# Moving the scale-and-round pass and the cap of a fake quantisation from VectorE to GpSimd in a chain of convolution layers

## The chip, the cores and the metric

The kernel runs on one core of a Trainium2 chip. The metric is the device time of one execution, in microseconds (us). The core has five engines that run side by side: TensorE (PE, with its weight loads shown as PEld), VectorE (DVE), ScalarE (ACT), GpSimd (POOL) and SyncE (SP), which here issues the DMAs. Each works through its own queue in order, and they wait for each other on semaphores.

## The reference, cut to what matters

The input is `x` of shape (4, 16, 512, 512). Four layers follow each other. Layer 0 is a windowed attention block. Layer 1 is what the change touches: its input is quantised with one step for the whole tensor, convolved, normalised with the mean and variance of the whole result, and clipped to 0..6.

```python
# layer 1
qp = 127.0
step = max(abs(x)) / qp
xq = clip(round(x / step), -qp, qp) * step
y = conv3x3(xq, wq)                       # wq is quantised in the same way
inv = gamma * rsqrt(var(y) + 1e-5)        # mean, var over batch, height, width
y = y * inv + (beta - mean(y) * inv)
y = clip(y, 0.0, 6.0)
# layer 2
out = conv3x3(relu(conv3x3(y, w1) + b1), w2) + b2 + y
# layer 3
out = out + w2 @ relu(w1 @ conv3x3(out) + b1) + b2
```

## The kernel before, in words

The image is cut into M = 64 pairs of rows per strip. A tile of the chain holds 128 partitions (4 strips or batches, 2 rows, 16 channels) by S = 4 by W = 512 fp32 elements, which is 2048 elements in each partition and 1 MiB in all.

The work has three stages. First, `window_attention` computes layer 0 and writes it to the DRAM tensor `x1`, in 64 steps. It also collects the largest absolute value in `peak`. Second comes the statistics pass at the head of `conv_layers` (L992 to L1014). Since layer 1 normalises with statistics of the whole convolution, its convolution is first computed for every tile only to collect them. Third comes the tail (the loop over `t` at the end of `conv_layers`), in which layers 1, 2 and 3 run as one pipeline, tile by tile, with the layer-1 convolution computed again.

In the statistics pass each of the 65 tiles (0 to 64) takes this path:

- `load` (L978; the DMAs at L891 to L895, issued by SP) brings the tile from `x1`. There are four buffers: two with the tag `x`, two with the tag `o`. A new load waits until the rounding has finished with the buffer.
- `scaled` (L984) multiplies the tile in place by the inverse step `ix` and adds `ROUND` = 12582912, which rounds to an integer in fp32.
- `rounded` (L987) subtracts `ROUND` on ACT and writes bf16 into one of three `qs` buffers.
- 24 turns of four matmuls (`_conv_turn`, L908) convolve tiles mm and mm+1 into four PSUM banks; two sets of banks alternate.
- `bn_stats` on DVE (L1009) reads the four banks.

Behind the last tile come the tiles -2 and -1 of the tail, whose first or last part lies outside the image and is set to zero by a memset (L888). Then `bn_aggr` (L1031) combines the statistics on DVE, and some ten tiny steps make `scale` and `shift` of it. Nothing of the tail's layer 1 can leave PSUM before.

In the tail one step `t` has four groups, each of them one convolution of 24 turns with the hidden layer of layer 3 (L1117, evacuated at L1123 on ACT and L1125 on DVE) laid between its turns, and the output product of layer 3 (L1131, L1137) at its end:

- group 1 is the convolution of layer 3, and between its turns the caps `clipped(t-1)` (L1060, one call per bank, with a memset at L1062 for tiles at the image's edge);
- group 2 is the second convolution of layer 2, and between its turns `scaled(t+2)` in four pieces of 512 elements, then `rounded(t+2)` in four;
- group 3 is the first convolution of layer 2, which reads the capped `z` of tiles t-2 and t-1;
- group 4 is the convolution of layer 1, after which `done0(t)` (L1054, ACT) writes `z` of tile t with scale, shift and ReLU. `done2` (L1084, DVE) later adds that `z` to the result of layer 2.

The order on PE, DVE, ACT and SP is the order in which the program text issues the instructions (a manual schedule, L961). POOL is not in that list: the framework's scheduler orders it. Before the change POOL holds a few memsets and three kinds of partition reduction, and nothing in the tail.

Of the kernel before, what the change touches and what calls it, by code (L numbers as in the profile page):

```python
# [14 lines left out]
ALU = mybir.AluOpType  # L15
# [20 lines left out]
ROUND = 12582912.0  # L36
BN_EPS = 1e-5
ACT_MAX = 6.0
# [813 lines left out]
def quant_step(nc, pool, out, columns, name):  # L852

    most = pool.tile([P, 1], F32, name=f"most_{name}")
    nc.vector.tensor_reduce(most, columns, AX.X, ALU.max, apply_absolute_value=True)
    every = pool.tile([P, 1], F32, name=f"every_{name}")
    nc.gpsimd.partition_all_reduce(every, most, P, bass_isa.ReduceOp.max)
    step = out.tile([P, 1], F32, name=f"step_{name}")
    nc.vector.tensor_scalar(step, every, 1.0 / QP, None, ALU.mult)
    inv = out.tile([P, 1], F32, name=f"inv_{name}")  # L860
    nc.vector.reciprocal(inv, step)
    return step, inv
# [17 lines left out]
def _quad(i):  # L880
    return slice(32 * i, 32 * i + 32)
# [34 lines left out]
def conv_layers(ctx: ExitStack, tc, x1, out, cw, cq, sw, m, v, peak):  # L916
# [18 lines left out]
    nc = tc.nc  # L935
# [33 lines left out]
    def inner(t):  # L969
        return t[:, :, 1 : W + 1]  # L970

    def outside(mm):

        return 0 if mm < 0 else S - 1 if mm >= M else None
# [6 lines left out]

    def scaled(mm, at=slice(0, S)):
        t = loaded[mm][:, at]
        nc.vector.tensor_scalar(t, t, ix, ROUND, ALU.mult, ALU.add)  # L984

    def rounded(mm, at=slice(0, S)):
        nc.scalar.activation(  # L987
# [7 lines left out]
    sx, ix = quant_step(nc, act, act, peak, "x")  # L995
    for mm in range(2):
        scaled(mm)
        rounded(mm)
    for mm in range(M):
        if mm + 4 <= M:  # L1000
            load(mm + 4, tags[mm % 2])
        if mm + 2 <= M:
            scaled(mm + 2)
            rounded(mm + 2)
        p = banks[4 * (mm % 2) : 4 * (mm % 2) + 4]
        for turn in _turns():
            _conv_turn(nc, p, cq, (qs(mm), qs(mm + 1)), *turn)
        for b in range(B):
            nc.vector.bn_stats(stats[:, mm * B + b, :], p[b])  # L1009
    for mm in (-2, -1):  # L1010
        load(mm)
        scaled(mm)
        rounded(mm)
# [43 lines left out]

    def clipped(mm, b):
        z = inner(zs(mm))
        nc.vector.tensor_scalar(z[:, b], z[:, b], ACT_MAX, None, ALU.min)  # L1060
        if outside(mm) is not None:
            nc.vector.memset(z[_quad(outside(mm)), b], 0.0)  # L1062

    def done1(mm):
        h = inner(hs(mm))
# [103 lines left out]
    for t in range(-2, M + 7):  # L1169
        if t + 3 <= M + 2:  # L1170
            load(t + 3)
        new = [lambda s=s: scaled(t + 2, slice(s, s + 1)) for s in range(S)]
        new += [lambda s=s: rounded(t + 2, slice(s, s + 1)) for s in range(S)]
        clip = [lambda b=b: clipped(t - 1, b) for b in range(B)]
        mm = t - 4
        group(
            conv(2, xs, mm - 1, done3, mm) if 0 <= mm <= M else None,
            (t - 6, 3) if 0 <= t - 6 < M else None,
            clip if -2 <= t - 1 <= M + 1 else [],
        )  # L1180
        mm = t - 3
        group(
            conv(1, hs, mm, done2, mm) if -1 <= mm <= M else None,
            (t - 5, 0) if 0 <= t - 5 < M else None,
            new if t + 2 <= M + 2 else [],
        )
        if -1 <= mm <= M:
            turned(mm)
        mm = t - 1
        group(  # L1190
            conv(0, zs, mm - 1, done1, mm) if -1 <= mm <= M + 1 else None,
            (t - 5, 1) if 0 <= t - 5 < M else None, [],
        )
        mm = t
        group(
            conv(None, qs, mm, done0, mm) if -2 <= mm <= M + 1 else None,
            (t - 5, 2) if 0 <= t - 5 < M else None, [],
        )
# [133 lines left out]
```

## Time and profile before

| what | value |
|---|---|
| median of three runs | 6609.31 us (6609.27 to 6616.03) |
| the profiled execution's own time | 6619.37 us |
| its span | 6617.5 us, mean granted clock 0.98 |
| PE busy | 6388.5 us, 97% of the span |
| ACT busy | 4209.4 us, 64% |
| DVE busy | 3192.7 us, 48% |
| POOL busy | 5.9 us |
| statistics pass | about 3560 to 3804 us in the span |
| tail | from there to the end |

The page of the profile cuts the span into 40 slices and shows for each the busy share of every engine in tenths. Rows of groups give the line of the kernel, the engine, the operation, the tiles (output <- input), their shapes, the number of instructions, busy time and mean duration of one in nanoseconds, and then the idle time of the engine before them with what ended it. Rows in order of time give the start and the duration. A row of busy time by stretch gives the stretch, its length, and each engine's busy time in it.

### The profile page before, as it was taken

How to read it: one execution, taken by the hardware profiler on the slowest of the kernel's cores; microseconds unless marked ns; L12 is line 12 of the kernel's file. 1: busy time of each engine (PE TensorE's matmuls, PEld its weight loads, DVE VectorE, ACT ScalarE, POOL GpSimd, SP SyncE). 2: the span in 40 equal slices, each digit the busy share in tenths (PEclk: the TensorE clock that was granted, in tenths of full speed). 3: DMA queues.
4: the chain of work that ended last, by engine and by line, in shares of the span. 5: the costliest groups of instructions: out<-in, count | busy, mean ns of one | idle time of the engine just before them, and what ended most of it. 6: DMA issues, size and time to landing. Idle time of an engine off the chain costs nothing. (4 is left out here: it accounts for less than half of the span.)

```text
span 6617.5 us, 317160 instructions
## 1 busy us (share of the span) xinstructions
PE 6388.5 (97%) x146976; PEld 3295.4 (50%) x146976; DVE 3192.7 (48%) x4640; ACT 4209.4 (64%) x5738; POOL 5.9 (0%) x25
## 2 busy tenths in 40 slices
PE   8999999999999999999996689999999999999998
PEld 5555555555555555555553344444444444444443
DVE  3444444444444444444445944444444444444444
ACT  5777777777777777777774545554555555555553
POOL 0000000000000000000000000000000000000000
PEclk9999999999999999999997789999999999999999
DMA  3333232333333333333324722222222222222221
GB/s 81 65 67 76 57 75 59 73 60 72 60 72 60 72 61 70 62 70 62 70 44 165 275 85 79 79 79 76 76 78 78 78 78 75 75 79 79 79 63 47
DMA packets 544391, 515.30 MB, mean 78 GB/s; under 512 B 349008, under 2 KB 480208, under 8 KB 514384
## 3 DMA queue, kind: packets, MB, share of 16 engines
q1 hardware_dynamic: 542768, 494.52, 28.6%
q8 instruction: 1154, 18.91, 1.2%
q14 instruction: 181, 1.48, 0.1%
q10 hardware_dynamic: 288, 0.39, 0.0%
HBM read 225.87 MB, written 134.48 MB: 54 GB/s over the span
## 5 line engine op out<-in xcount | busy, mean ns | idle before, releaser
L1117 PE MATMUL tb<-y,mat 32*32 32x512 f32 x16384 | 1684.6, 597 | 14.0 <-ACT hid L1123 7.5
L1123 ACT ACTIVATE hid<-tb,vec 128x512 f32<-128x512 f32 x1280 | 877.0, 687 | 1231.0 <-PE tb L1117 1205.6
L1125 DVE TENSOR_SCALAR hid<-tb,vec 128x512 f32<-128x512 f32 x768 | 576.8, 751 | 1173.9 <-PE tb L1117 860.5
L367 ACT ACTIVATE e<-pair 128x1024 f32<-128x1024 f32 x1024 | 992.4, 1021 | 225.7 <-PE pair L359 225.0
L295 PE MATMUL pair<-x,taps 32*32 32x512 f32 x18432 | 968.1, 606 | 1.9 <-ACT y L306 1.3
L416 PE MATMUL bank<-y,fc_e 32*32 32x512 f32 x8192 | 878.4, 607 | 3.7 <-ACT hid L421 3.1
L421 ACT ACTIVATE hid<-bank,f1b 128x512 f32<-128x512 f32 x1024 | 679.3, 686 | 298.3 <-PE bank L416 284.6
L351 DVE COPY yt<-bank 128x512 f32<-128x512 f32 x512 | 353.7, 691 | 905.8 <-PE bank L346 905.5
L1117 PEld LDWEIGHTS tb<-y,mat 32*32 32x32 f32 x16384 | 500.3, 103 | 406.0 <-issue 242.8
L359 PE MATMUL pair<-g,y 32*128 32x128 f32 x16384 | 652.2, 285 | 39.7 <-ACT e L367 38.7
L908 PE MATMUL tb<-z,cw 32*32 32x512 f32 x12864 | 643.8, 603 | 4.0 <-ACT z L1054 3.4
L359 PEld LDWEIGHTS pair<-g,y 32*128 32x128 f32 x16384 | 541.4, 186 | 185.9 <-ACT e L367 108.8
L908 PE MATMUL tb<-x,cw 32*32 32x512 f32 x12480 | 632.0, 597 | 1.5 <-ACT z L1054 1.5
L908 PE MATMUL tb<-h,cw 32*32 32x512 f32 x12672 | 628.6, 601 | 1.8 <-ACT z L1054 1.5
L295 PEld LDWEIGHTS pair<-x,taps 32*32 32x32 f32 x18432 | 459.0, 103 | 288.8 <-issue 183.7
L908 PE MATMUL tb<-q,cq 32*32 32x512 bf16 x12672 | 446.5, 436 | 122.1 <-ACT q L987 97.9
L378 PE MATMUL bank<-e,yt 128*32 128x128 f32 x16384 | 555.3, 276 | 0.9 <-ACT r L393 0.9
L383 PE MATMUL bank<-e,hot 128*32 128x512 f32 x4096 | 534.4, 592 | 0.0
L1131 PE MATMUL tb<-hid,mat 128*32 128x512 f32 x4096 | 498.5, 605 | 0.9 <-DVE o L1137 0.9
L378 PEld LDWEIGHTS bank<-e,yt 128*32 128x32 f32 x16384 | 417.7, 109 | 108.1 <-DVE yt L351 52.8
L429 DVE TENSOR_TENSOR xo<-bank,y 128x512 f32<-128x512 f32 x256 | 177.1, 692 | 546.2 <-PE bank L427 544.4
L346 PEld LDWEIGHTS bank<-mat,y 128*128 128x128 f32 x2048 | 215.2, 141 | 430.2 <-issue 376.5
(150 smaller groups left out, 6608.8 us busy)
## 6 DMA issues: line engine op xcount, KB each, us to landing
tx<-x SPq DMA_DIRECT2D x128, 1024.0 KB, 5.2
x<-in_xw_dram SPq DMA_DIRECT2D x32, 2600.0 KB, 9.9
y<-y SPq DMA_DIRECT2D x2048, 32.0 KB, 2.2
xi<-x SPq DMA_DIRECT2D x1024, 64.0 KB, 2.8
out_dram<-o SPq DMA_DIRECT2D x64, 1024.0 KB, 4.1
x<-xo SPq DMA_DIRECT2D x2000, 32.0 KB, 1.7
tx<-x SPq DMA_DIRECT2D x4, 768.0 KB, 4.2
x<-xo SPq DMA_DIRECT2D x48, 24.0 KB, 1.6
```

The costliest lines, as they stand in the source:

```text
L295: nc.tensor.matmul(bank(u)[quad(vv)], taps[quad(u), tap, :], xts[n // 2][quad(u), vv, dy : dy + WS, at : at + BW], start=tap == 0, stop=ta ...
L359: nc.tensor.matmul(bank(u)[:, P * jj : P * jj + P], y2[quad(u), vv, jl + jj].rearrange("p w t -> p (w t)"), g[quad(u), vv, jl + jj].rearra ...
L367: nc.scalar.activation(e[:, 2 * i : 2 * i + 2].rearrange("p u j t -> p u (j t)"), pairs[i], AF.Exp,)
L378: nc.tensor.matmul(b[quad(u), P * jj : P * jj + P], yt[:, jj, quad(u)], e[:, u, jj, :], start=True, stop=True,)
L383: nc.tensor.matmul(d[quad(u)], own, e[:, u].rearrange("p j t -> p (j t)"), start=True, stop=True,)
L416: nc.tensor.matmul(b[quad(k)], fc1[quad(vv), quad(k)], y[quad(vv), u, :], start=True, stop=True,)
L421: nc.scalar.activation(hd, b, AF.Gelu, bias=f1b)
L908: nc.tensor.matmul(p[i][_quad(j)], weights[_quad(i), side, dx, :], src[side][_quad(i), j, dx : dx + W], start=side == 0 and dx == 0, stop= ...
L1117: nc.tensor.matmul(p[_quad(c)], w1[_quad(b), 1 - par, 32 * c : 32 * c + 32], inner(ys(mm + par))[_quad(b), s, :], start=True, stop=True,)
L1123: nc.scalar.activation(hd, p, AF.Relu, bias=v("l3_b1"))
L1125: nc.vector.tensor_scalar(hd, p, v("l3_b1"), 0.0, ALU.add, ALU.max)
L1131: nc.tensor.matmul(out_bank[_quad(b), :], w2[:, par], hd, start=par == 0, stop=par == 1)
```

## The change

The scale-and-round pass of `scaled`, the cap of `clipped` and the memset behind the cap are issued on GpSimd. `scaled` serves both the statistics pass, with 2048 elements at a time, and the tail, with 512. Operands, types and the places in the program text stay as they were.

```diff
     def scaled(mm, at=slice(0, S)):
         t = loaded[mm][:, at]
-        nc.vector.tensor_scalar(t, t, ix, ROUND, ALU.mult, ALU.add)
+        nc.gpsimd.tensor_scalar(t, t, ix, ROUND, ALU.mult, ALU.add)
...
     def clipped(mm, b):
         z = inner(zs(mm))
-        nc.vector.tensor_scalar(z[:, b], z[:, b], ACT_MAX, None, ALU.min)
+        nc.gpsimd.tensor_scalar(z[:, b], z[:, b], ACT_MAX, None, ALU.min)
         if outside(mm) is not None:
-            nc.vector.memset(z[_quad(outside(mm)), b], 0.0)
+            nc.gpsimd.memset(z[_quad(outside(mm)), b], 0.0)
```

## The prediction

> **What bounds the kernel now.** I read the page's forty slices first, to see which stages there are, then busy time by stretch, then the groups and the order of time inside the stage that the change touches.
>
> ```profile
> PE   8999999999999999999996689999999999999998
> DVE  3444444444444444444445944444444444444444
> POOL 0000000000000000000000000000000000000000
> DMA  3333232333333333333324722222222222222221
> ```
>
> PE fills every slice but three, and only in those does VectorE (DVE) reach 9. They are the statistics pass. Busy time by stretch (engines in the order PE, PE weight load, DVE, ACT, POOL, then granted clock, DMA share, GB/s) puts figures on it:
>
> ```profile
> 3564.00:3576.00 12.00, 6.39 (x238) 3.86 (x238) 7.73 (x9) 6.09 (x4) 0.00 (x0) 0.57 1.01 422
> 3590.00:3790.00 200.00, 128.97 (x5308) 76.00 (x5284) 198.44 (x276) 110.27 (x55) 0.00 (x0) 0.77 0.82 292
> 3960.00:6500.00 2540.00, 2535.49 (x60055) 1113.48 (x60043) 1222.29 (x1939) 1282.62 (x1935) 0.00 (x0) 1.00 0.24 76
> ```
>
> In the pass (second row) DVE works 198.4 of 200 us and PE 129: DVE sets the pace. In the tail (third row) PE works 2535.5 of 2540 us and DVE under half: there a lighter DVE can give back at most the 4.5 us in which PE idles. The first row is the start of the pass, when four loads are waiting: DMA is full and moves 422 GB/s. The groups of the pass's steady part and two of its rounds in order of time:
>
> ```profile
> L1009 DVE BATCH_NORM_STATS2 stats<-tb 128x6 f32<-128x512 f32 x220 | 136.8, 684 | 1.6 <-PE tb L908 0.3
> L987 ACT ACTIVATE q<-tx,unround 128x2048 bf16<-128x2048 f32 x55 | 110.3, 2005 | 89.9 <-DVE tx L984 53.4 <-PE tb L908 36.5
> L984 DVE TENSOR_SCALAR tx<-tx,inv_x 128x2048 f32<-128x2048 f32 x56 | 71.1, 1270 | 0.0
> ...
> 3593.07 1.27 DVE L984 TENSOR_SCALAR tx<-tx,inv_x 128x2048 f32<-128x2048 f32 x1
> 3594.26 2.48 DVE L1009 BATCH_NORM_STATS2 stats<-tb 128x6 f32<-128x512 f32 x4
> 3596.66 1.27 DVE L984 TENSOR_SCALAR tx<-tx,inv_x 128x2048 f32<-128x2048 f32 x1
> ```
>
> A round is 3596.66 - 3593.07 = 3.59 us: one scale-and-round pass, 1.19 us from start to start, and four bn_stats, 2.40 us (they overlap a little). ACT's rounding, 2.0 us a tile, waits 53.4 us on L984. Scaling starts at 3564.8 (tile 0), and tile 64's ends at 3797.9: 65 tiles in 233 us, 3.59 us each.
>
> What POOL does is in one row that can serve as a price:
>
> ```profile
> L279 POOL MEMSET y<- 128x4096 f32 x1 | 3.5, 3516 | 0.0
> ```
>
> **What the Trainium skill says.** (1) GPSIMD Engine Reference, 3.1 (Elementwise): a body of up to two operations is bound by the read and write ports at 1.03 cycles an element, a good loop of more work by 1.8; a two-input tensor_tensor on 2048 fp32 elements takes 4497 ns, some 2.6 cycles. With the page's clock of 1.2 GHz the first is 0.86 ns an element; the memset above took 3516/4096 = 0.86 ns, so that the trace agrees, for a write without a read. No run here shows a GpSimd tensor_scalar. (2) The same page, 4.1 (Engine selection): work with one input is "roughly line-rate" on GpSimd. (3) SBUF — State Buffer, "Who interferes with whom": GpSimd shares a port pair with VectorE, taken as a lock by VectorE's two-port modes and two-SBUF-input operations; tensor_scalar can enter those modes. 2048 elements in 1.27 us on L984, against 512 from PSUM in 0.75 us on L1125, fit that. Just these SBUF-to-SBUF passes leave DVE. What stays reads PSUM with at most one SBUF operand (bn_stats, hidden, done2, output), so I charge no lock; no run here shows one.
>
> **The change part by part.**
>
> Removed from DVE: 65 passes of 128x2048 in the pass and two more for tiles -2 and -1; in the tail four scalings (L984, 479 ns) and four caps (L1060, 420 ns) per step, 3.6 us of a step of about 38 us, and 16 memsets at the edges (L1062). No DMA and no PE or ACT instruction moves. POOL's queue gets them all, in the order pass tiles, then per step four scalings and four caps; it issues no DMA, so nothing but these stands behind a wait in it. In DVE's queue the waits for a landed tile go too.
>
> Pass, on the path. Without L984, DVE needs 2.40 us a tile. What is next: DMA, 1.05 MB at 422 GB/s = 2.48 us; PE, where two convolutions back to back took 4.88 us at 3570.6, 2.44 us each, at a granted clock of about 0.6 to 0.7; ACT 2.0 us and its waits; POOL, unknown. The four tile buffers allow one tile per quarter of load + scale + round: (5.1 us landing + 1.9 + 2.0 + about 0.5 of signals)/4 = 2.4 us. Four limits of 2.4 to 2.5 us that hand over to each other won't be met exactly; I take 2.7 us, with 2.45 as the floor and 3.0 as the ceiling if POOL stays out of the way.
>
> POOL's pass over 2048 elements, bounded from both sides: below by the memset's rate, 2048 x 0.86 = 1.76 us; above by the tensor_tensor price, 4.5 us, or worse if each operation is a pass of its own. I take 1.9 us: one input, two operations and no second read, which is what the skill's first price describes, with 0.1 us for the start. It then matters little whether it is 1.8 or 2.5: POOL decides only from 2.5 us on, and the change loses only from 3.59 us on.
>
> Sum: tile 64 is scaled at 3564.8 + 65 x 2.7 = 3740.3 instead of 3797.9: -57.6 us.
>
> End of the pass. The last bn_stats end at 3803.5; on DVE follow memset, scaling, memset, scaling, and only at 3807.14 the 7.08 us aggregation on which everything hangs. Both scalings leave, the two memsets stay: it starts about 2.5 us earlier. POOL scales those tiles beside the aggregation. -2.5 us.
>
> First steps of the tail. The rounding of tile 0 waits at 3818.1 for the DVE queue; POOL can do the scaling during the aggregation: up to -1 us. In the first two steps POOL has scalings, caps and memsets together, about 8 x 0.5 + 4 x 0.5 = 6 us in a step of 7.5 us: 0 to +2 us. Taken as 0.
>
> Steady tail. Eight POOL passes per step: at 0.55 us each (512 x 0.86 ns and a start) 4.4 us, at 1.2 us 10 us, of 38 us. The cap follows done0 at the end of step t-1 and is read by conv 0 in the third group of t, two groups or some 19 us later; a tile is loaded a step before its scaling, which POOL may do ahead of ACT's rounding. Both are covered by PE's work even at the slow price. On DVE the relief lies where it waits for PE anyway. 0, at best -4 us.
>
> Total -60 us. The profiled execution took 6619.4 us (span 6617.5), so it would be 6559; it lies 10 us above the median of the three runs, 6609.3, and no part of the change touches what differs. Against the median: **about 6549 us**, -0.9%. What is late next in the pass is the loads and PE, in turn.
>
> **Rivals.**
>
> A. GpSimd at about 1.8 cycles an element (the skill's price for a good loop of more work): 3.07 us and a start, 3.17 a tile, and POOL becomes the bound of the pass. 3564.8 + 65 x 3.17 = 3770.9, -27 us, and -2.5: 6580. For it: GpSimd runs a software loop. Against: the memset's rate and "line-rate".
>
> B. GpSimd at the tensor_tensor price, slower than before. One mechanism: POOL's pass takes over 3.59 us, the round of today; ACT then waits for POOL where it waited for DVE, PE for ACT, and DVE idles. At 4.44 us and a start, 4.5: 3564.8 + 65 x 4.5 = 3857.3, +59 us, -2.5, and up to +3 in the first tail steps, in which the 12 passes and memsets outgrow the step: 6667. For it: two arithmetic steps with a per-partition operand, of which the trace has no example. Against: only one tensor is read. Were the two operations two loops (7 us a tile) it would be near 6825.
>
> C. The pass keeps its 3.6 us because buffers or the rounding bind there: -2.5 us, 6607. Against: DVE has 1.6 us of idle time in 200 and DMA has run at 422 GB/s on the same loads.
>
> **How the numbers follow.** Forecast 0.46, A 0.22, B 0.22 with 0.05 more for still slower, C 0.05. The forecast's own range is 6533 (2.45 us a tile) to 6568 (3.0 us). A measurement of this kernel can tell about 0.2%, 13 us, from no change. Faster by more is the forecast and A, with some of A's slow end gone: 0.67; within it 0.06; slower 0.27. The forecast and A alone hold under seven in ten, so the range must reach over B: 6533 to 6668, which leaves out what is slower than B.
>
> **What would show it.** In the changed profile, L984 stands on POOL with 128x2048 passes of 1.8 to 2.0 us from start to start when nothing holds it, DVE in the pass falls from 99% to about 89% of a shorter time (2.4 of 2.7), DMA rises from 0.82 to over 0.9, and the aggregation starts within 1.3 us of the last bn_stats. ACT L987 would wait on PE or on landing loads, not on L984. If POOL's passes stand back to back, with ACT waiting for them, A or B is right, by their length. The tail's PE share stays at 99.8% with the granted clock at 1.00; if ACT L987 or conv 0 waits for POOL there, the cover that I named is wrong.

## The result, and the profile after

The changed kernel takes 6646.6 us (median of five runs, 6642.1 to 6649.6) against 6613.1 us for the kernel before (five runs). The ratio is 1.0045, with a 95% interval of 1.0033 to 1.0057: **slower by 0.45%**, where the prediction had 0.9% faster. The profiled execution has a span of 6645.2 us, 27.7 us more than before.

The same four rows of slices as before, of the changed kernel:

```profile
PE   8999999999999999999995679999999999999999
DVE  3444444444444444444444624444444444444443
POOL 0000000000000000000002442222222222222210
DMA  3333232333333333333224722222222222222221
```

DVE has left its 9, and POOL carries 4 in the pass and 2 in the tail: the work has moved as it should. But the dip of PE is as wide as it was. Busy time by stretch for the steady part of the pass and for the tail (columns as in the prediction):

```profile
3590.00:3790.00 200.00, 124.35 (x4992) 82.13 (x4992) 128.54 (x208) 103.75 (x53) 107.76 (x55) 0.72 0.77 284
3960.00:6500.00 2540.00, 2539.63 (x60145) 1120.76 (x60119) 1044.12 (x1453) 1282.08 (x1932) 524.82 (x484) 1.00 0.24 77
```

In the pass nothing is full any more. DVE went from 198 to 129 us of 200, POOL works 108, PE 124, ACT 104, and the DMA share fell from 0.82 to 0.77. The number of tiles done in 200 us fell as well: 53 roundings against 55. The groups of that stretch say who waits for whom:

```profile
L1009 DVE BATCH_NORM_STATS2 stats<-tb 128x6 f32<-128x512 f32 x208 | 128.5, 684 | 70.3 <-PE tb L908 69.9
L908 PE MATMUL tb<-q,cq 32*32 32x512 bf16 x4992 | 124.3, 520 | 74.1 <-issue 71.4 <-DVE stats L1009 2.6
L984 POOL TENSOR_SCALAR tx<-tx,inv_x 128x2048 f32<-128x2048 f32 x55 | 108.8, 1977 | 93.8 <-DMA tx<-x 86.0 <-ACT q L987 7.9
L987 ACT ACTIVATE q<-tx,unround 128x2048 bf16<-128x2048 f32 x53 | 105.7, 2004 | 94.9 <-PE tb L908 84.7 <-POOL tx L984 10.2
```

GpSimd's pass takes 1977 ns, close to the 1.9 us taken for it. DVE and ACT wait for PE, POOL waits for loads, whose buffers ACT frees. PE itself waits 71.4 us for "issue", which means for nothing that another engine did. In order of time its matmuls have a pattern:

```profile
3685.00 2.07 PE L908 MATMUL tb<-q,cq 32*32 32x512 bf16 x128 [1.94 <-issue]
3689.84 3.61 PE L908 MATMUL tb<-q,cq 32*32 32x512 bf16 x128 [2.77 <-issue]
3694.68 2.08 PE L908 MATMUL tb<-q,cq 32*32 32x512 bf16 x128 [1.23 <-issue]
```

PE runs 128 matmuls, stops, and runs 128 more; in these lines the starts are 4.84 us apart, elsewhere more or less. A convolution has 96, so the stops have nothing to do with tiles. Each matmul has a weight load of its own (4992 of each in the 200 us), which makes 256 instructions a burst. The DMA queues of the same 200 us (packets, MB, share of 16 engines), of the kernel before and after:

```profile
q8 instruction: 41, 0.67, 1.3%
...
q8 instruction: 39, 0.64, 1.2%
```

39 packets of 16.4 KB in 200 us are one in 5.1 us, and 39 times 256 is just the 4992 matmuls and 4992 weight loads: each packet is a block of 256 instructions of PE. The Trainium skill (Runtime: NRT & Kernel Launch, Instruction fetch mechanics) describes such blocks: an engine's instructions are refilled in 16 KiB blocks of 256 through a DMA queue of their own, and it calls the cost mostly hidden. The trace agrees on the blocks. On the cost it agrees in the tail, where 74 packets came in the 400 us from 4000 on, one in 5.4 us, and PE was busy throughout. In the pass the measurement differs: PE could use a block up in 2.1 to 3.6 us, and the next one comes after some 5.

Where the 27.7 us of span went, by marks found in both traces:

| stretch | before, us | after, us | difference |
|---|---|---|---|
| start of the program to the first load of the pass | 3559.8 | 3564.9 | +5.1 |
| to the first scaling | 5.0 | 12.2 | +7.2 |
| to the end of the last bn_stats | 238.7 | 250.6 | +11.9 |
| to the aggregation | 3.6 | 1.0 | -2.6 |
| to the end of `shift` | 11.1 | 12.4 | +1.3 |
| to DVE's first L1077 (first steps of the tail) | 19.8 | 30.1 | +10.3 |
| to DVE's last L1077 (the steady tail) | 2675.4 | 2672.0 | -3.4 |
| to the end | 104.1 | 102.1 | -2.0 |

The first row lies ahead of everything that was changed, and the same mark stands at 3555.6 in one kernel below that has GpSimd in the pass (e5) and at 3565.8 in another (e12): it varies by itself. The tail's row varies too: 2675.4, 2669.2 and 2675.1 us in the kernel before, e5 and e11, which have the same tail.

Three more rows of the changed kernel on POOL's new work: its wait ahead of the first scaling, its mean price, and that of the cap.

```profile
3577.08 3.92 POOL L984 TENSOR_SCALAR tx<-tx,inv_x 128x2048 f32<-128x2048 f32 x2 [11.15 <-issue]
...
L1060 POOL TENSOR_SCALAR z<-z 128x512 f32<-128x512 f32 x272 | 404.5, 1487 | 139.9 <-ACT z L1054 118.2
L984 POOL TENSOR_SCALAR tx<-tx,inv_x 128x512 f32<-128x512 f32 x268 | 181.6, 697 | 1951.7 <-DMA tx<-x 1355.0 <-ACT z L1054 560.1 <-ACT hid L1123 36.1
```

### The profile page after: what moved, and what is told of

The parts are those of the page before. It is cut to its first block, busy times and chain, and to the rows that moved or that the text cites. A ratio compares the mean times of both kernels' runs of the same rounds, so it can differ in the third digit from the quotient of the medians.

```text
span 6645.2 us, 317620 instructions
## 1 busy us (share of the span) xinstructions
PE 6391.7 (96%) x146976; PEld 3308.3 (50%) x146976; DVE 2910.1 (44%) x4017; ACT 4209.7 (63%) x5738; POOL 732.4 (11%) x648
## 5 line engine op out<-in xcount | busy, mean ns | idle before, releaser
L984 POOL TENSOR_SCALAR tx<-tx,inv_x 128x512 f32<-128x512 f32 (+1 forms) x333 | 310.1, 947 | 2067.8 <-DMA tx<-x 1452.1
```

## The experiments

Theory F: PE's instruction blocks pace the pass at about 5 us for 128 matmuls. Rival H: the hand-over load, scale, round is too long for its four buffers. Later rivals are named where they come up. F was formed on the profiles of before and after; the experiments test it. "Pass" in the table is the stretch from the first to the last start of a bn_stats in the profiled execution, divided by the 64 tiles; the ratio is to the kernel before on the same chip.

| kernel | median, us | before, us | ratio (95%) | pass, us a tile |
|---|---|---|---|---|
| before | | 6613.1 | | 3.60 |
| changed | 6646.6 | 6613.1 | 1.0045 (1.0033 to 1.0057) | 3.79 |
| e1_no_scale | 6631.7 | 6620.3 | 1.0016 (1.0010 to 1.0023) | 3.80 |
| e2_third_of_pe | 6582.3 | 6620.3 | 0.9949 (0.9932 to 0.9965) | 2.81 |
| e3_three_buffers | 6647.4 | 6620.3 | 1.0047 (1.0030 to 1.0064) | 3.73 |
| e4_six_buffers | 6645.5 | 6620.3 | 1.0043 (1.0027 to 1.0060) | 3.85 |
| e5_pass_only | 6635.0 | 6616.3 | 1.0027 (1.0017 to 1.0036) | 3.79 |
| e6_tail_only | 6627.2 | 6616.3 | 1.0019 (1.0010 to 1.0028) | 3.60 |
| e7_no_reload | 6651.9 | 6616.3 | 1.0056 (1.0039 to 1.0073) | 3.76 |
| e8_quarter_columns | 6643.2 | 6616.3 | 1.0043 (1.0026 to 1.0060) | 3.72 |
| e9b_half_loads | 6599.2 | 6615.1 | 0.9974 (0.9962 to 0.9985) | 3.30 |
| e10_pairs_before | 6621.9 | 6615.1 | 1.0009 (1.0000 to 1.0017) | 3.57 |
| e11_pairs_pass_only | 6577.7 | 6615.1 | **0.9943** (0.9927 to 0.9960) | 2.81 |
| e12_pairs_after | 6587.1 | 6615.1 | 0.9955 (0.9939 to 0.9972) | 2.82 |

**e1_no_scale: could anything have been won?** The kernel before, with the scaling taken out of the pass altogether.

```diff
         if mm + 2 <= M:
-            scaled(mm + 2)
             rounded(mm + 2)
```

> The kernel before with the scaling of the 65 tiles of the statistics pass left out altogether (so the statistics are those of other numbers). Theory F (PE's instruction fetch paces the pass: 192 instructions a tile come in blocks of 128 matmuls with their weight loads, one block per about 5 us while the loads fill the DMA engines): the pass keeps 3.6 to 3.75 us a tile, only the end of the pass moves, 6600 to 6620 us against 6613 before. Theory H (the hand-over load, scale, round with its four buffers is too long): one stage less shortens it, about 2.6 us a tile, near 6550.

With no scaling on any engine the pass takes 3.80 us a tile, and the kernel is 0.16% slower than before (the interval leaves out 1). Taking all scaling off DVE was thus worth nothing. F named this outcome, but both its ranges, 3.6 to 3.75 us a tile and 6600 to 6620 us, were a little too low. The stretch that corresponds to the one above has the same half-empty engines.

```profile
3590.00:3790.00 200.00, 127.13 (x5120) 84.95 (x5120) 129.64 (x210) 105.33 (x53) 0.00 (x0) 0.72 0.75 279
```

H would have had 6550 us and is wrong by 80 us. GpSimd is cleared too, since it does nothing in this pass, which is as slow as the changed kernel's.

**e2_third_of_pe: fewer instructions.** The changed kernel with a third of the pass's matmuls.

```diff
         for turn in _turns():
-            _conv_turn(nc, p, cq, (qs(mm), qs(mm + 1)), *turn)
+            if turn[:2] in ((0, 0), (1, 2)):
+                _conv_turn(nc, p, cq, (qs(mm), qs(mm + 1)), *turn)
```

> The changed kernel with only 2 of 6 taps in the convolution of the statistics pass (32 matmuls a tile instead of 96, other statistics), all else as it was. Theory F: a third of the instructions, so fetch no longer binds; 2.5 to 2.8 us a tile, 60 to 75 us faster than the changed kernel's 6646: 6570 to 6590. Theory H: loads, scaling and rounding are the same, so about 3.7 us a tile and 6640.

2.81 us a tile, 6582 us. Its pass, and its instruction queue in 150 us of it:

```profile
3600.00:3750.00 150.00, 65.66 (x1724) 18.70 (x1724) 131.54 (x213) 106.48 (x54) 105.01 (x54) 0.50 0.97 373
```

```profile
q8 instruction: 14, 0.23, 0.7%
```

Now DMA is full (0.97), and GpSimd's 1.98 us a tile is hidden. So PE held the pass, by its instructions or by its own work, which e8 separates.

**e3 and e4: the buffers.** The changed kernel with three buffers under one tag, and with three for each of the two tags, with as many loads ahead.

```diff
-        loaded[mm] = ld.tile([P, S, W], F32, tag=tag, name=f"tx{mm}")
+        loaded[mm] = ld.tile([P, S, W], F32, tag="x", name=f"tx{mm}", bufs=3)    # e3
+        loaded[mm] = ld.tile([P, S, W], F32, tag=tag, name=f"tx{mm}", bufs=3)    # e4
```

> The changed kernel with three tile buffers in the statistics pass instead of four. Theory F: fewer loads are queued ahead of an instruction block, blocks come no later and perhaps earlier: 3.3 to 3.75 us a tile, 6620 to 6646. Theory H: (6.2 us landing + 2 + 2 + 0.5)/3 = 3.6 at the very least and in fact more, since four gave 3.75 where (10.7)/4 = 2.7 was the bound: up to 5 us a tile, 6650 to 6720.

> The changed kernel with six tile buffers in the statistics pass instead of four. Theory F: no gain, as more loads stand ahead of an instruction block: 3.7 to 4.2 us a tile, 6645 to 6675. Theory H: the path is covered, 2.6 to 2.8 us a tile, 6575 to 6590.

3.73 and 3.85 us a tile against 3.79: the number of buffers hardly matters, either way. (In time e3, at 6647.4 us, lies just above F's range.) H expected a difference of a microsecond or more on each side.

**e8_quarter_columns: instructions, or TensorE's work?** As many matmuls, each a quarter as long.

```diff
-            _conv_turn(nc, p, cq, (qs(mm), qs(mm + 1)), *turn)
...
+            for j in range(4):
+                nc.tensor.matmul(p[i][_quad(j), 0:128], cq[_quad(i), side, dx, :],
+                    (qs(mm), qs(mm + 1))[side][_quad(i), j, dx : dx + 128], ...
```

> The changed kernel with as many matmuls in the statistics pass as it has, each of 128 columns instead of 512 (the rest of the banks is zero, so other statistics). Theory F (instruction blocks): as many instructions, so the pass keeps 3.5 to 3.8 us a tile, 6630 to 6650. Theory P (what the third of the matmuls relieved was TensorE's own work, at a granted clock of 0.7 to 0.8, not its instructions): 2.5 to 2.8 us a tile, 6570 to 6590.

3.72 us a tile. PE's bursts are shorter and its stops longer:

```profile
3690.75 1.56 PE L1010 MATMUL tb<-q,cq 32*32 32x128 bf16 x128 [1.38 <-issue]
3695.87 1.59 PE L1010 MATMUL tb<-q,cq 32*32 32x128 bf16 x128 [3.55 <-issue]
```

These two starts are 5.12 us apart, and 40 instruction packets in 200 us make 5.0 us each, as with the long matmuls. With e2 this settles it: the pass is paced by the number of PE's instructions and not by how much they do. The granted clock does not decide it either, since it is 0.50 both in e2 and here.

**e9b_half_loads: does a block wait behind the loads?** e1 with half of each tile loaded.

```diff
-            load(mm + 4, tags[mm % 2])
+            loaded[mm + 4] = loaded[mm]
+            nc.sync.dma_start(loaded[mm + 4][:, 0:2], x1[mm + 4, :, 0:2])
...
```

> The kernel before without scaling in the statistics pass, as in e1_no_scale, and with only half of each tile loaded there from the fifth tile on (the other half keeps what an earlier tile left; other statistics). Theory F1 (an instruction block of 16 KB is late because it queues behind the tile loads): with half the bytes the blocks come sooner, 2.4 to 3.0 us a tile, 40 to 75 us faster than before. Theory F2 (a block takes about 5 us whatever else the DMA engines do): 3.6 to 3.8 us a tile as in e1_no_scale, within 15 us of before.

The result lies between the two theories, in neither's range: 3.30 us a tile, 0.26% faster than before. In 150 us there were 34 instruction packets, one in 4.4 us, at a DMA share of 0.49. Fewer bytes of loads bring a block sooner, but by 0.7 of e1's 5.1 us (39 packets in 200 us); most of the 4.4 us remains with the DMA engines half idle. A packet itself kept a DMA engine busy for about 1 us (an estimate: 1.2% of the time of 16 engines in 200 us, over 39 packets). What the rest consists of stays open; the run halves the bytes of the loads but not the number of their packets (6480 in 150 us, 7587 in 200 us of e1), so that a wait behind packets is not excluded.

**e5 and e6: the two parts of the change alone.**

```diff
-        nc.gpsimd.tensor_scalar(t, t, ix, ROUND, ALU.mult, ALU.add)
+        engine = nc.gpsimd if at == slice(0, S) else nc.vector    # e5; e6: the other way round
+        engine.tensor_scalar(t, t, ix, ROUND, ALU.mult, ALU.add)
```

The line taken out is that of the changed kernel. In e5 the cap and its memset are on VectorE, in e6 on GpSimd.

> GpSimd scales only the 2048-element tiles of the statistics pass (and -2, -1); the scalings of 512 elements and the cap with its memsets are on VectorE as before. From the terms of the two profiles: +7 us until GpSimd's first scaling (its library reload), +12 us in the pass, -2.6 us at its end, nothing from the tail: 15 to 20 us slower than before. If instead the tail's first steps are not what GpSimd slows, it stays at the changed kernel's distance, 27 to 33 us.

> The other part alone: VectorE scales in the statistics pass, GpSimd scales 512 elements at a time and caps in the tail. From the terms: +1 us in the tiny VectorE steps, +9 to +11 us in the first tail steps (caps of 1.49 us each on GpSimd), -4 us in the steady tail: 5 to 10 us slower than before. If the pass is the only cause, within 3 us of before.

The pass's part costs 18.8 us (6635.0 - 6616.3), as expected. The tail's costs 10.9 us, a little over the 5 to 10 expected. Together that is 29.7 us, and the whole change costs 33.5 by its medians, 30 by its ratio: the two parts add up. From the end of `shift` to the first L1077's counterpart (first steps of the tail) it is 21.0 us in e5 and 28.0 in e6, against 19.8 before, so most of the tail's loss lies there.

**e7_no_reload: the wait before the first scaling.** In the changed kernel two MODIFY_POOL_CONFIG stand between GpSimd's partition reduction and the first L984, and an idle time of 11.15 us that ends without anything to wait for. I take it for the reload of GpSimd's library. Here a tiny tensor_scalar asks for it earlier, and the maximum is found without the partition reduction.

```diff
+    warm = wts.tile([P, 1], F32, name="warm")
+    nc.gpsimd.tensor_scalar(warm, ytop, 1.0, None, ALU.mult)
...
-    sx, ix = quant_step(nc, act, act, peak, "x")
+    nc.tensor.transpose(banks[7][0:1, 0:P], most, m("ident"))
+    nc.vector.tensor_reduce(high, banks[7][0:1, 0:P], AX.X, ALU.max)
+    nc.tensor.matmul(banks[6][:, 0:1], one, high, start=True, stop=True)
...
```

> The changed kernel with the maximum for the quantisation step taken over partitions by a transpose on TensorE and a reduction on VectorE, and a one-element GpSimd tensor_scalar ahead of the stage, so that GpSimd's library reload is done before the first tile lands. If the 11 us reload is exposed as the profile has it, 6 to 8 us faster than the changed kernel. If PE's instruction blocks set the start of the pass as well, under 2 us.

The wait did move with the first tensor_scalar: it ends at 3544 and is 6.96 us instead of 11.15. Now the first scaling comes 5.0 us after the first load instead of 12.2. The aggregation starts at 3817.1 instead of 3828.6. Yet the kernel is no faster than the changed one, where 6 to 8 us faster had been expected: from the first to the last L1077 the tail takes 2685.3 us against 2672.0. The tail's instructions are the same, and the extra time is spread over all its steps. Its cause stays open, so what the reload costs the whole kernel is not shown by this run.

**e10, e11, e12: half the instructions for the same sums.** Two batches stand on the diagonal of 64 by 64 weights, so that 48 matmuls do what 96 did.

```diff
+    cp = act.tile([P, 2, 3, 64], BF16, name="cp")    # zero, then cq twice on the diagonal
...
-        for turn in _turns():
-            _conv_turn(nc, p, cq, (qs(mm), qs(mm + 1)), *turn)
+        for side, dx, half, r, c in ...:
+            rows = slice(64 * r, 64 * r + 64)
+            nc.tensor.matmul(p[2 * r + half][64 * c : 64 * c + 64], cp[rows, side, dx, :],
+                             src[side][rows, 2 * half + c, dx : dx + W], ...
```

> The kernel before with the convolution of the statistics pass in 48 matmuls of 64 rows by 64 columns of weights (two batches on the diagonal) instead of 96 of 32 by 32: the same sums, half the instructions, twice the streaming time on TensorE. VectorE still scales, and sets 3.6 us a tile: within 6 us of before. If TensorE at its granted clock needs more than 3.6 us a tile for them, slower by 10 us or more.

> The same 48 matmuls, and GpSimd scales in the statistics pass only, as in e5_pass_only. Theory F: instruction blocks no longer bind (one per 2.7 tiles), so that what GpSimd takes off VectorE shows: 2.7 to 3.2 us a tile, 20 to 50 us faster than before, that is faster than both kernels. If TensorE's own time binds (2.6 us at full clock, 3.4 at 0.75): 3.4 us or more a tile, -5 to +10 us.

> The changed kernel in full with the same 48 matmuls: e11 and the tail's part of the change on GpSimd. 8 to 14 us more than e11_pairs_pass_only, by the first tail steps.

Alone (e10) the new matmuls give nothing: the ratio is 1.0009, 6.8 us slower by the medians, and the pass takes 3.57 us a tile, with VectorE working 149.8 of 150 us. With GpSimd scaling in the pass (e11) it is 2.81 us a tile and 6577.7 us, 37 us under before: **faster than both kernels**. In its pass every resource is well used, and DMA is full:

```profile
3600.00:3750.00 150.00, 140.00 (x2528) 90.34 (x2524) 130.97 (x211) 105.05 (x54) 103.75 (x53) 1.00 0.97 367
```

Who waits in e11 (waited for; us in total, times, longest): GpSimd for loads, ACT for GpSimd, and PE's weight loads (PEld) for instructions, now and then.

```profile
ACT q L988 <- POOL tx L985: 45.3, 51, 2.8
POOL tx L985 <- DMA tx<-x: 40.6, 50, 2.8
PEld L1020 <- issue: 15.7, 19, 2.1
```

Weight loads by themselves are not the limit that fell: PEld works 90 of 150 us here and 82 of 200 in the changed kernel.

The whole change on top of the new matmuls (e12) costs 9.4 us more than e11, within the expected 8 to 14. Against e10 it gains 35 us: with the instructions out of the way, the same change is faster by half a per cent.

## Why the prediction was wrong, point by point

**The step that failed** is "PE, where two convolutions back to back took 4.88 us at 3570.6, 2.44 us each", and with it the list of four limits and the 2.7 us a tile. The two convolutions were the first of the pass, run without a stop for instructions. In the steady pass of the changed kernel PE gets 128 matmuls in about 5 us, 3.8 us a tile, which the list left out. The term "-57.6 us" measured +11.9 from the first scaling to the last bn_stats. By the prediction's own mark, the end of tile 64's scaling, it was +0.3 (233.4 us against 233.1); the convolutions fell behind the scaling, so that the last bn_stats ended 17.2 us after it instead of 5.6.

A sign stood in the profile of before. PE's matmuls waited mostly for ACT, but in part for "issue", and the first such stop came right behind the two convolutions that I had taken for the price:

```profile
L908 PE MATMUL tb<-q,cq 32*32 32x512 bf16 x5308 | 130.1, 484 | 71.0 <-ACT q L987 56.2 <-issue 14.0
...
3577.78 2.74 PE L908 MATMUL tb<-q,cq 32*32 32x512 bf16 x82 [2.28 <-issue]
```

The 41 instruction packets in 200 us of before, one per 4.9 us, were what 3.6 us a tile needs, so they did not show by themselves that no more could come. I took the idle shares of the other engines for slack. e10 and e1 give the two bounds: VectorE holds the pass at 3.57 us a tile when instructions are few, and the instruction blocks hold it at 3.80 when VectorE has no scaling.

**Why slower, and not only no gain,** stays open. Before, the blocks kept up with 3.6 us a tile; in the changed kernel and in e1 they gave no better than 3.8. The loads come less evenly there: in slices of 5 us from 3600 to 3790 the DMA share lies between 0.7 and 0.9 before and swings between 0.4 and 0.9 in the changed kernel. No run tests whether that delays the blocks.

**Rival C** ("the pass keeps its 3.6 us because buffers or the rounding bind there") came nearest in the pass, but by luck: e3 and e4 exclude the buffers, and it had the kernel a little faster, not slower. Its argument against, that DVE had 1.6 us of idle time in 200, shows only that DVE was a limit, not that it was the only one. Rivals A and B fell: GpSimd takes 1.98 us for 2048 elements.

**GpSimd's price** was right, 1.98 us against 1.9 taken. The port-bound price of the Trainium skill (GPSIMD Engine Reference, 3.1, Elementwise), an estimate of 1.76 us for 2048 elements, lies 0.2 us under it. The 2.7 us a tile was right too, as what the other resources allow: 2.81 in e2, e11 and e12, with DMA at 0.97.

**End of the pass**: -2.5 expected, -2.6 found.

**The library reload** was missing from the sum. The Trainium skill (GPSIMD Engine Reference, 2.1, Instruction dispatch) states about 6 us for the first call after a library is loaded; here GpSimd waited 11.15 us before its first scaling, which came 12.2 us after the first load, where DVE's had come after 5.0.

**First steps of the tail**: 0 to +2 us expected, +10.3 in the marks; e6 and the difference of e12 and e11 give 10.9 and 9.4. The term was mis-sized because the cap was priced like the scaling: 0.5 us, where it takes 1.49 us for 512 elements, twice the 0.70 us of the scaling of as many. Four caps, four memsets (0.52 us each) and four scalings make 10.8 us in steps of 7.5. ACT's rounding waits for them, and PE for ACT and for a memset behind a cap:

```profile
3852.25 0.72 ACT L987 ACTIVATE q<-tx,unround 128x512 bf16<-128x512 f32 x1 [6.21 <-POOL tx L984]
...
3854.91 8.52 PE L908 MATMUL tb<-z,cw 32*32 32x512 f32 x102 [7.30 <-ACT z L1054]
3865.20 5.11 PE L908 MATMUL tb<-z,cw 32*32 32x512 f32 x77 [1.77 <-POOL z L1062]
```

**Steady tail**: 0 to -4 us expected. The marks give -3.4, within what equal tails vary by. The cover named there held: PE works 2539.6 of 2540 us.

**The port lock**: I charged none, and for the large operation of the pass that was right (a bn_stats takes 684 ns before and after). But the tiny steps between aggregation and `shift` include tensor_tensor with two SBUF inputs, and GpSimd was scaling beside them. The changed kernel's row for two of them, 160 ns each before:

```profile
L1027 DVE TENSOR_TENSOR mul_v<-os_var,mul_s x1: 633/633/633, 3838.0 to 3838.0; 128x1 f32<-128x1 f32 x1
L1027 DVE TENSOR_TENSOR mul_v<-mul_v,mul_s x1: 636/636/636, 3838.6 to 3838.6; 128x1 f32<-128x1 f32 x1
```

That is what the Trainium skill (SBUF — State Buffer, "Who interferes with whom") says of two-SBUF-input operations beside a GpSimd read, and with the `scale` step (0.54 us) it makes up the +1.3 us. In e5, whose GpSimd does not scale beside these steps, the stretch takes 11.0 us, against 11.1 before.

## What to carry to other kernels

Before work is taken off the engine that is full, ask what each of the other engines and queues would need at the hoped-for rate, and count PE's instructions among these needs: this stage needed a 16 KB block for every 128 matmuls with their weight loads, and a block took about 5 us. Here the limit showed as idle time of PE put down to "issue" between bursts of 128 matmuls, and fewer, larger matmuls relieved it although they stream longer. A run that leaves the suspected work out altogether tells cheaply whether moving it can pay.

## What the runs showed of the hardware that had not been expected

- Where PE waited for them, blocks of 256 PE instructions came every 5.0 to 5.1 us in this pass with the DMA engines 75 to 78% busy (changed kernel, e1, e8), and every 4.4 us at 49% (e9b).
- On GpSimd a two-operation tensor_scalar (multiply, add) took 697 ns for 512 elements and 1977 ns for 2048, which is 0.83 ns an element and some 270 ns of start; a one-operation min with a constant on 512 elements took 1487 ns. Whether operation, operand or the tile's offset makes the difference was not tried.
- GpSimd's wait before its first tensor_scalar, taken for the library reload, was 11.15 us beside the tile loads and 6.96 us ahead of them (e7).
